# The first routing stage of a macaron block on one core: earlier rows of the second token group, the first group's residual on VectorE, paired statistics, fewer warm-up products

## The chip, the cores and the metric

The kernel runs on one core of a Trainium2 chip. The core has TensorE (PE: matrix products; PEld is its weight load), VectorE (DVE), ScalarE (ACT), GpSimd (POOL) and SyncE (SP), which here only issues DMAs. Each engine works through its own instruction list in order and waits on semaphores. The metric is the device time of one execution in microseconds (us). The inputs lie in HBM, and the output goes back there.

## The reference, cut to what matters

The input `x` is 16 x 256 tokens of 256 channels, float32. The block is

```
x = x + 0.5 * ffn(LN(x))     # mixture of experts
x = x + attention(LN(x))
x = x + 0.5 * ffn(LN(x))     # the same weights again

ffn(h):                      # h is LN(x)
  n    = w_norm * h / sqrt(mean(h*h) + 1e-6)
  p    = softmax(n @ w_router)             # 32 experts; the 4 best of each token
  out  = sum over the chosen experts of p * (silu(n@w_gate[e]) * (n@w_up[e])) @ w_down[e]
  out += sigmoid(n @ w_shared_gate) * ((silu(n@sw_gate) * (n@sw_up)) @ sw_down)
  return h + out
```

Since `ffn` returns `h + out`, the first line is `x + LN(x)/2 + out/2`. The change touches the beginning of this first line: the statistics of `LN`, the sum `x + LN(x)/2`, and the order in which rows and weights come in.

## The kernel before

The 4096 tokens are 32 tiles of 128 rows, in 8 groups (g = 0 to 7) of 4 tiles. All of `x` stays in one on-chip tile `x` [128, 32, 256].

**Loads.** SP issues in this order: group 0 of `x` in two halves (`load_x(0, 2)`, L116), the identity matrix `kc` (L119), `wnorm` (L134), the router's weights `wr` (L136, L137), the shared expert's gate and up weights `sw` in four pieces (gate columns 0 to 639, gate 640 to 703, up 0 to 639, up 640 to 703; L144, L145), group 1 of `x` (L146, recorded as L116), the down weights `swd` (L148, L151), then groups 2 to 7 of `x` (L153). All of them go through one hardware queue.

**Routing of a group,** `route(n, g, rows)` (n = 0 is the first feed-forward), is a generator, and each `yield` lets other work in between:

1. `moments(g)`: for each tile `bn_stats` (L221) and `bn_aggr` (L222) on DVE give mean and variance `mv`. `root` on POOL (L228, then a power of -1/2 at L229) turns the variance into `s2` (for the normed rows) and `s1` (for the LayerNorm). POOL then makes the factors `xa` (L242) and `xb` (L244, L245) of `x + LN(x)/2 = xa*x + xb`.
2. DVE writes the normed rows `xr` (L250), 4 instructions.
3. Twice (h = 0, 1): PE transposes two tiles of `xr` into PSUM (`pt`, L267), and ACT scales them into `xnT` (L270).
4. `mixed()` writes `x = xa*x + xb` over `x`, 4 instructions of ACT (L258). It overwrites `x`, so it stands after `xr`. For the first group it is written after the router's exponential (L294), for the other groups between the two halves of step 3.
5. PE makes the router's logits `pl` (L283). DVE, ACT and DVE again make the softmax, the four best experts and the mask (L287 to L316). The table of rows `xtab` goes to HBM (L308).

**The shared expert of a group,** `shared`, is what PE is filled with in the meantime: for each of 6 column chunks k, gate and up products into two PSUM tiles `pg` (L402, `sw` times `xnT`), a tanh on ACT (L407; L430 for the last chunk), and two products on DVE (L408 and L420; L432 and L433 for the last chunk). Then the down products `po` (L457) for four tiles, each added to `x` by DVE (L461). `po` needs all six chunks `act`.

**What sets the order.** PE runs in the order in which the code is written (`tc.manual_schedule(engines={ET.PE})`, L101). On DVE, ACT, POOL and SP a planner orders the first stage: it goes through the program once with costs of its own and gives each engine the earliest written instruction that it believes to be ready. The list is then fixed; on the chip an instruction that waits holds up everything behind it on its engine. A `manual_schedule` region for DVE fixes the written order among the DVE instructions in it, and leaves to the planner where other DVE work falls between them.

**Warm-up.** `warm(count)` issues products of zeros on PE (L190): 9 before the first transposes, and 3 between the transposes of group 0 and its logits (`WARM = (9, 3)`, L739 and L740). Each float32 product shows as two records in the profile.

In `feed_forward` (L728) the written order for g = 0 is: first half of step 3 for group 0, `moments` of group 1, second half of step 3, `xr` of group 1, the warm-up, logits of group 0 and their softmax, `moments` of group 2; after that the first chunk of the shared expert. `advance(first[0], 2)` (L791) has written steps 1 and 2 of group 0 before that.

Of the kernel before, what the change touches and what calls it, by code (L numbers as in the profile page):

```python
# [9 lines left out]
F32 = mybir.dt.float32  # L10
BF16 = mybir.dt.bfloat16
I32 = mybir.dt.int32
AF = mybir.ActivationFunctionType
ALU = mybir.AluOpType
# [4 lines left out]
P = 128  # L19
# [3 lines left out]
GT = 4  # L23
# [16 lines left out]
ET = mybir.EngineType  # L40
# [3 lines left out]
ROUTE_FILL, SLOT_FILL, FIRST_FILL, EXPERT_FILL, SUM_FILL, PROJECT_FILL = 3.0, 1.7, 6.0, (2.15, 2.3), 17.0, 1.5  # L44
LAST_FILL = 8.0
MASK_FILL, ROW_FILL = 4.0, 3.2
WARM = (9, 3)
AHEAD = 3
SPARE = (0.0, 0.0, 2.0, 3.0)
LAST = 4 * (NG - 1)  # L50
# [43 lines left out]
def macaron_kernel(ctx: ExitStack, tc: tile.TileContext, X, Wq, Wk, Wv, Wo, w_norm, w_router, w_gate, w_up,  # L94
                   w_down, sw_gate, sw_up, sw_down, w_shared_gate, consts, out):
    nc = tc.nc
# [14 lines left out]
    x = cpool.tile([P, NT, C], F32, name="x")  # L111

    def load_x(g, parts=1):
        for i in range(g * GT, (g + 1) * GT, GT // parts):
            j = i + GT // parts
            nc.sync.dma_start(x[:, i:j, :], xf[i * P : j * P, :].rearrange("(t p) c -> p t c", p=P))  # L116
# [23 lines left out]
    sw = cpool.tile([P, 2, 2 * FS], F32, name="sw")  # L140
    swv = [w.rearrange("(c p) f -> p c f", p=P) for w in (sw_gate, sw_up)]
    f0 = FC[-1][0]
    for s in range(2):
        nc.sync.dma_start(sw[:, :, s * f0 : (s + 1) * f0], swv[s][:, :, 0:f0])  # L144
        nc.sync.dma_start(sw[:, :, 2 * f0 + s * FR : 2 * f0 + (s + 1) * FR], swv[s][:, :, f0:FS])  # L145
    load_x(1)  # L146
    swd = cpool.tile([P, len(FC), C], F32, name="swd")
    nc.sync.dma_start(swd[:, 0:5, :], sw_down[0:640, :].rearrange("(c p) d -> p c d", p=P))  # L148

# [66 lines left out]
    def moments(g):  # L216

        mv = stat.tile([P, GT, 2], F32, name="mv", bufs=5)
        for t in range(GT):
            st = stat.tile([P, 6], F32, name="st")  # L220
            nc.vector.bn_stats(st, x[:, g * GT + t, :])  # L221
            nc.vector.bn_aggr(mv[:, t, :], st)  # L222
        return mv

    def root(name, mv, scale, add):
# [6 lines left out]
    def route(n, g, rows):  # L232

        mv = moments(g)


        s2 = root("s2", mv, 1.0 + RMS_EPS, RMS_EPS * LN_EPS)
        s1 = root("s1", mv, 1.0, LN_EPS)  # L240
        xa = stat.tile([P, GT], F32, name="xa", bufs=5)
        nc.gpsimd.tensor_scalar(xa, s1, 0.5, 1.0, ALU.mult, ALU.add)  # L242
        xb = stat.tile([P, GT], F32, name="xb", bufs=5)
        nc.gpsimd.tensor_mul(xb, s1, mv[:, :, 0])  # L244
        nc.gpsimd.tensor_scalar_mul(xb, xb, -0.5)  # L245
        yield 0.0
        xr = rows.tile([P, GT, XW], F32, name="xr", bufs=2 if n else 3)
        for t in range(GT):
            i = g * GT + t
            nc.vector.tensor_scalar(  # L250
                xr[:, t, 0:C], x[:, i, :], mv[:, t, 0:1], s2[:, t : t + 1], ALU.subtract, ALU.mult
            )
        yield 0.0

        def mixed():
            for t in range(GT):
                i = g * GT + t
                nc.scalar.activation(  # L258
                    x[:, i, :], x[:, i, :], AF.Identity, bias=xb[:, t : t + 1], scale=xa[:, t : t + 1]
                )  # L260

        for h in range(GT // 2):
            pt = ps1.tile([P, 2, 2, P], F32, tag="mm", name="pt")
            for j in range(2):
                t = 2 * h + j
                for c in range(2):
                    nc.tensor.transpose(pt[:, c, j, :], xr[:, t, c * P : (c + 1) * P], ident)  # L267
            i0 = (g * GT + 2 * h) * P
            for c in range(2):
                nc.scalar.activation(  # L270
                    xnT[:, c, i0 : i0 + 2 * P], pt[:, c].rearrange("p j t -> p (j t)"), AF.Identity,
                    scale=wnorm[:, c : c + 1],
                )
            yield 0.5
            if h == 0:
                if n or g:
                    mixed()
                yield 0.0
        pl = ps1.tile([P, GT, E + 1], F32, tag="mm", name="pl")
        for t in range(GT):  # L280
            i = g * GT + t
            for c in range(2):
                nc.tensor.matmul(  # L283
                    pl[:, t, :], lhsT=xnT[:, c, i * P : (i + 1) * P], rhs=wr[:, c, :], start=(c == 0), stop=(c == 1)
                )
        lg = stat.tile([P, GT, E + 1], F32, name="lg", bufs=2)
        nc.vector.tensor_copy(lg, pl)  # L287
        nc.vector.tensor_copy(gate[:, g * GT : (g + 1) * GT], lg[:, :, E])
        mx = stat.tile([P, GT, 1], F32, name="mx")
        nc.vector.tensor_reduce(mx[:, :, 0], lg[:, :, 0:E], AX.X, ALU.max)  # L290
        ex = stat.tile([P, GT, E], F32, name="ex", bufs=2)
        nc.vector.tensor_sub(ex, lg[:, :, 0:E], mx.to_broadcast([P, GT, E]))
        yield 1.9
        nc.scalar.activation(ex, ex, AF.Exp)  # L294
        if n == 0 and g == 0:
            mixed()
        yield 0.0
        tot = stat.tile([P, GT, 1], F32, name="tot")
        nc.vector.tensor_reduce(tot[:, :, 0], ex, AX.X, ALU.add)
        nc.vector.reciprocal(tot, tot)  # L300

        pr = stat.tile([P, GT, E + 4], F32, name="pr", bufs=1)
        nc.vector.memset(pr[:, :, E : E + 4], -1.0)
        nc.vector.tensor_mul(ex, ex, tot.to_broadcast([P, GT, E]))

        nc.vector.scalar_tensor_tensor(pr[:, :, 0:E], ex, TINY, ex, ALU.is_ge, ALU.mult)
        nc.gpsimd.tensor_copy(xr[:, :, C:XW], pr[:, :, 0:E])
        nc.sync.dma_start(xtab[n][g * GW : (g + 1) * GW, :].rearrange("(t p) c -> p t c", p=P), xr)  # L308
        top = stat.tile([P, GT, 8], F32, name="top")
        hit = stat.tile([P, GT, E + 4], F32, name="hit", bufs=1)  # L310
        for t in range(GT):
            nc.vector.max(top[:, t, :], pr[:, t, 0:E])
        nc.vector.memset(top[:, :, TOPK:8], -1.0)
        for t in range(GT):
            nc.vector.match_replace(hit[:, t, :], top[:, t, :], pr[:, t, :], 2.0)
        nc.vector.tensor_single_scalar(  # L316
            mask[:, :, g * GT : (g + 1) * GT], hit[:, :, 0:E].rearrange("p t e -> p e t"), 1.5, ALU.is_gt
        )
        yield 0.0
# [360 lines left out]
    def advance(work, count=1):  # L680
        for _ in range(count if work else 0):
            next(work, None)
# [45 lines left out]
    def feed_forward(n, pool, works, fill, routed=None):  # L728


        for g, work in works.items():
            later = [works.get(g + d) for d in range(3)]
            next(work)
            if g == 0:
                next(later[1])
            fill.take(ROUTE_FILL)
            advance(work, 2)
            advance(later[1])
            if n == 0 and g == 0:  # L739
                warm(WARM[1])  # L740
            fill.take(ROUTE_FILL)
            advance(work, 2)
            advance(later[2])
            fill.ready = g + 1
            fill.take(ROUTE_FILL)
            next(work)
        if n == 0:
            routed.close()
            clear(0)
            load_attention()  # L750
        idx = pool.tile([P, E], I32, name="idx")
        fill.take(MASK_FILL)
        with tc.tile_pool(name=f"slots{n}", bufs=4, side="right", reuse_waits="tile") as sp:
            works = [slots(sp, idx, q) for q in range(E // 8)]
            for step in range(5):
                for w in works:
                    next(w)
                    fill.take(SLOT_FILL if step < 3 else ROW_FILL)
        fill.take(FIRST_FILL)
        wds = [pool.tile([FE, 2, C], F32, name=f"wd{i}") for i in range(3)]  # L760
        for wd in wds:
            nc.gpsimd.memset(wd[FR:FE, 1, :], 0.0)
        steps = [expert(pool, n, e, idx, wds[e % 3]) for e in range(E)]


        twice = pool.tile([P, C], F32, name="twice")
        for h in range(2):
            nc.sync.dma_start(twice[h * FR : (h + 1) * FR, :], sw_down[640:FS, :])
        fill.paired = twice

        for e in range(AHEAD):
            next(steps[e])
        fill.halves = True
        with tc.manual_schedule(engines={ET.Pool}):
            for e in range(E + 2):
                if e + AHEAD < E:
                    next(steps[e + AHEAD])
                for late in range(3):
                    if 0 <= e - late < E:
                        next(steps[e - late], None)  # L780
                fill.take(EXPERT_FILL[n])
        fill.halves = False
# [4 lines left out]
    with tc.tile_pool(name="ffn0", bufs=1) as pool:  # L787
        rows0 = ExitStack()
        xrows = rows0.enter_context(tc.tile_pool(name="rows0", bufs=3, side="right"))
        first = {g: route(0, g, xrows) for g in range(NG)}  # L790
        advance(first[0], 2)  # L791
        feed_forward(0, pool, first, fill, rows0)
        if n == 0:
            fill.paired = None
# [174 lines left out]
```

## Time and profile before

| | us |
|---|---|
| median of 3 runs (lowest to highest) | 1030.83 (1030.72 to 1031.55) |
| the profiled execution | 1031.41 |
| its span, first to last instruction | 1029.5 |
| PE busy | 1012.2 (98%) |
| DVE busy | 640.2 (62%) |
| POOL busy | 496.4 (48%) |
| ACT busy | 410.1 (40%) |

The start of the execution, in stretches (busy us of each engine, DMA as the mean busy share of 16 DMA engines and GB/s):

| stretch, us | PE | DVE | ACT | POOL | DMA share | GB/s |
|---|---|---|---|---|---|---|
| 5 to 10 | 5.00 | 1.68 | 2.23 | 3.21 | 0.98 | 324 |
| 10 to 15 | 4.84 | 2.19 | 3.28 | 0.79 | 1.11 | 335 |
| 15 to 20 | 4.68 | 4.33 | 2.17 | 2.62 | 1.10 | 348 |
| 20 to 25 | 5.00 | 4.36 | 2.75 | 3.22 | 1.02 | 344 |
| 25 to 30 | 5.00 | 4.66 | 2.93 | 0.32 | 0.74 | 199 |
| 30 to 35 | 5.00 | 4.32 | 2.46 | 3.10 | 0.14 | 48 |
| 35 to 40 | 4.71 | 3.60 | 2.04 | 2.41 | 0.84 | 218 |
| 40 to 50 | 7.83 | 9.94 | 3.99 | 5.01 | 0.94 | 292 |
| 50 to 60 | 10.00 | 5.31 | 2.52 | 5.11 | 0.94 | 314 |

A line of the timeline or of the chain begins with the start and the length in us, then the engine, the line of the code and the operation; "x4" is how many instructions were merged, and the bracket at the end of a timeline's line is the idle time before it and what ended it. A line of the waits reads: engine and line that waited, whom it waited for, then the total, the number and the longest wait. A matmul's end is modelled, so a busy PE is not always PE at its best rate.

### The profile page before, as it was taken

Reading aid. Unit: us, or ns where it says so; the run is one execution under the profiler, and the core shown is the slowest. Engines: PE = TensorE matmul, PEld = TensorE weight load, DVE = VectorE, ACT = ScalarE, POOL = GpSimd, SP = SyncE. Lnnn points to the kernel's source line nnn. Section 1 sums busy time; section 2 is a strip of 40 time slices with the busy share of each in tenths; the row PEclk is TensorE's granted clock in tenths of the full one; section 3 lists DMA queues with packets and bytes.
Section 4 is the critical chain, followed back from the end, with each engine's and each line's share of the span. In section 5 each row is a group of like instructions: output and inputs, shape, how many; then the busy total and the mean of one; then the engine's idle time right before and its main releaser. Section 6 shows DMA issues by size and latency. Waiting matters only on the chain.

```text
span 1029.5 us, 15832 instructions
## 1 busy us (share of the span) xinstructions
PE 1012.2 (98%) x5432; PEld 639.4 (62%) x5432; DVE 640.2 (62%) x1698; ACT 410.1 (40%) x896; POOL 496.4 (48%) x548
## 2 busy tenths in 40 slices
PE   9999999999999999999999999999999999999998
PEld 6657646777866464545555554555566477877755
DVE  5865665455453557787878879775755644454553
ACT  4442111223231247676758667667310123232210
POOL 4410101555553389788687767754100235555442
PEclk9999999999999999999999999999999999999999
DMA  9731801788873100000101010000310157788564
GB/s 297 215 125 47 249 8 50 167 176 176 179 159 47 46 22 3 20 21 2 44 1 45 1 44 13 12 24 2 105 33 1 35 119 170 170 174 177 104 174 169
DMA packets 138191, 93.26 MB, mean 91 GB/s; under 512 B 80576, under 2 KB 135424, under 8 KB 138112
## 3 DMA queue, kind: packets, MB, share of 16 engines
q1 hardware_dynamic: 125824, 74.42, 25.8%
q0 software_dynamic: 12288, 17.83, 10.5%
q8 instruction: 44, 0.72, 0.3%
q14 instruction: 35, 0.29, 0.1%
HBM read 61.25 MB, written 30.97 MB: 90 GB/s over the span
## 4 chain that ended last, share of the span: by engine, by line
PE 83%; DVE 7%; DMA 4%; POOL 3%; issue 1%; ACT 1%; SPq 0%; POOLq 0%; DVEq 0%
PE pg L402 26%; PE po L457 8%; PE pge L492 7%; PE pq L558 7%; PE poe L505 5%; PE poa L673 5%; PE sc L607 5%; PE pos L457 4%; PE y L655 3%; PE den L655 3%; PE pv L586 3%; DMA acc<-y,idx 2%; PE pl L283 2%; PE pte L484 1%; DVE xr L250 1%
## 5 line engine op out<-in xcount | busy, mean ns | idle before, releaser
L402 PE MATMUL pg<-xnT,sw 128*128 128x512 f32 x704 | 320.7, 596 | 0.5 <-DVE act L427 0.5
L402 PEld LDWEIGHTS pg<-xnT,sw 128*128 128x128 f32 x704 | 129.9, 190 | 130.6 <-issue 121.1
L508 POOL DMA_INDIRECT acc<-y,idx x64 | 101.4, 1584 | 178.1 <-DVE y L507 83.0
L407 ACT ACTIVATE act<-pg 128x512 f32<-128x512 f32 (+1 forms) x94 | 52.9, 563 | 206.4 <-PE pg L402 198.4
L614 ACT ACTIVATE p<-sc 128x512 f32<-128x512 f32 (+1 forms) x256 | 105.0, 497 | 74.9 <-PE sc L607 74.8
L408 DVE SCALAR_TENSOR_TENSOR act<-act,pg 128x512 f32<-128x512 f32 (+1 forms) x94 | 60.7, 646 | 80.1 <-ACT act L407 79.7
L457 PE MATMUL po<-swd,act 128*128 128x256 f32 x432 | 102.4, 385 | 4.4 <-ACT x L258 1.8
L468 POOL DMA_INDIRECT xg<-xtab,idx x64 | 68.1, 1064 | 73.9 <-DVE idx L377 55.0
L619 ACT ACTIVATE p<-p 128x512 f32<-128x512 f32 (+1 forms) x128 | 102.3, 867 | 0.0
L621 POOL TENSOR_SCALAR_AFFINE_SELECT p<-p 128x512 f32<-128x512 f32 x128 | 83.4, 676 | 36.6 <-ACT p L619 35.2
L492 PE MATMUL pge<-xgT,wgu 128*112 128x128 f32 (+1 forms) x768 | 95.0, 273 | 0.7 <-DVE sie L500 0.7
L457 PEld LDWEIGHTS po<-swd,act 128*128 128x128 f32 x432 | 79.6, 190 | 22.6 <-issue 6.0
L492 PEld LDWEIGHTS pge<-xgT,wgu 128*112 128x112 f32 (+1 forms) x768 | 88.9, 182 | 1.9 <-issue 1.9
L487 ACT ACTIVATE xgT<-pte,wnorm 128x128 f32<-128x128 f32 x128 | 40.0, 365 | 108.7 <-PE pte L484 108.7
L420 DVE TENSOR_TENSOR act<-act,pg 128x512 f32<-128x512 f32 x80 | 54.9, 687 | 29.7 <-PE pg L402 28.8
L498 DVE SCALAR_TENSOR_TENSOR sie<-sie,pge 112x256 f32<-112x256 f32 x64 | 27.0, 421 | 69.4 <-ACT sie L497 69.3
L566 POOL TENSOR_TENSOR qs<-qs,kc 128x512 f32<-128x512 f32 x48 | 61.4, 1280 | 9.8 <-DVE qs L561 9.8
L505 PE MATMUL poe<-wd,sie 112*128 112x256 f32 x256 | 66.0, 380 | 0.0
L457 PE MATMUL pos<-swd,act 128*128 128x256 f32 x280 | 63.8, 380 | 0.0
L673 PE MATMUL poa<-wo,yT 128*128 128x256 f32 x256 | 60.0, 386 | 1.4 <-DVE qT L565 1.4
L558 PE MATMUL pq<-hT,wq 128*128 128x512 f32 x128 | 60.9, 600 | 0.0
L607 PE MATMUL sc<-qT,kT 32*128 32x256 f32 (+1 forms) x512 | 59.9, 533 | 0.0
(118 smaller groups left out, 1478.5 us busy)
## 6 DMA issues: line engine op xcount, KB each, us to landing
xtab<-xr SPq DMA_DIRECT2D x16, 576.0 KB, 3.3
acc<-zero SPq DMA_DIRECT2D x2, 4224.0 KB, 15.9
a<-acc SPq DMA_DIRECT2D x16, 512.0 KB, 7.0
wgu<-in_L_ffn_w_gate SPq DMA_DIRECT2D x64, 112.0 KB, 2.7
wgu<-in_L_ffn_w_up SPq DMA_DIRECT2D x64, 112.0 KB, 2.9
wd<-in_L_ffn_w_down SPq DMA_DIRECT2D x64, 112.0 KB, 2.9
wgu<-in_L_ffn_w_gate SPq DMA_DIRECT2D x64, 64.0 KB, 2.8
wgu<-in_L_ffn_w_up SPq DMA_DIRECT2D x64, 64.0 KB, 2.8
```

The lines of the kernel that those rows point to most:

```text
L402: nc.tensor.matmul(pg[s], lhsT=sw[:, c, at[s] : at[s] + P], rhs=xnT[:, c, cols], start=(c == 0), stop=(c == 1))
L457: nc.tensor.matmul(po, lhsT=act[:, k, t * P : (t + 1) * P], rhs=swd[:, k, :], start=(k == 0 and paired is None), stop=(k == rest if paired ...
L468: nc.gpsimd.indirect_dma_start(out=xg, out_offset=None, in_=xtab[n], in_offset=bass.IndirectOffsetOnAxis(ap=idx[:, e : e + 1], axis=0), bo ...
L492: nc.tensor.matmul(pg[:fw, n_, :], lhsT=wgu[:, c, w0 : w0 + fw], rhs=xgT[:, c, :], start=(c == 0), stop=(c == 1))
L505: nc.tensor.matmul(po, lhsT=si[:, k, :], rhs=wd[:, k, :], start=(k == 0), stop=(k == 1))
L508: nc.gpsimd.indirect_dma_start(out=acc[n], out_offset=bass.IndirectOffsetOnAxis(ap=idx[:, e : e + 1], axis=0), in_=y, in_offset=None, boun ...
L558: nc.tensor.matmul(pq, lhsT=weights[:, c, :], rhs=hT[:, c, :], start=(c == 0), stop=(c == 1))
L607: nc.tensor.matmul(sc[i][:, 0 : 2 * w].rearrange("p (s t) -> p s t", s=2), lhsT=kT[r, m, t0 + k0 : t0 + k0 + P], rhs=qT[r, m, :, t0 + T - ...
L614: nc.scalar.activation(dst[:, i].rearrange("p s t -> p (s t)"), sc[i][:, 0 : 2 * w], AF.Tanh, scale=QK_SCALE / SOFTCAP)
L619: nc.scalar.activation(parts[h], parts[h], AF.Exp, scale=SOFTCAP)
L621: nc.gpsimd.affine_select(out=diag, in_=diag, compare_op=ALU.is_ge, fill=0.0, base=0, pattern=[[0, 4], [1, P]], channel_multiplier=-1,)
L673: nc.tensor.matmul(po, lhsT=yT[:, c // 2, c % 2, qh * P : (qh + 1) * P], rhs=wo[:, c // 2, c % 2, :], start=(c == 0), stop=(c == 3),)
```

## The change

1. `sw` comes in six pieces: columns 0 to 127 of gate and of up; then group 1 of `x`; then columns 128 to 639 of both; then 640 to 703 of both. Two DMAs more in all, the same bytes.
2. `moments` takes the tiles two at a time: two `bn_stats`, then two `bn_aggr`.
3. `mixed` of group 0 in the first feed-forward is 4 `tensor_scalar` of VectorE in place of 4 activations of ScalarE, at the same place in the written order.
4. `moments` and `xr` of group 0, its first transposes, and then `moments` of group 1 are written inside a region that fixes DVE's order. The order in which they were written is the same as before.
5. The second warm-up is 1 product, not 3.

```diff
-WARM = (9, 3)
+WARM = (9, 1)
...
     for s in range(2):
-        nc.sync.dma_start(sw[:, :, s * f0 : (s + 1) * f0], swv[s][:, :, 0:f0])
+        nc.sync.dma_start(sw[:, :, s * f0 : s * f0 + P], swv[s][:, :, 0:P])
+    load_x(1)
+    for s in range(2):
+        nc.sync.dma_start(sw[:, :, s * f0 + P : (s + 1) * f0], swv[s][:, :, P:f0])
+    for s in range(2):
         nc.sync.dma_start(sw[:, :, 2 * f0 + s * FR : 2 * f0 + (s + 1) * FR], swv[s][:, :, f0:FS])
-    load_x(1)
...
-        for t in range(GT):
-            st = stat.tile([P, 6], F32, name="st")
-            nc.vector.bn_stats(st, x[:, g * GT + t, :])
-            nc.vector.bn_aggr(mv[:, t, :], st)
+        for h in range(0, GT, 2):
+
+            sts = [stat.tile([P, 6], F32, name="st") for _ in range(2)]
+            for d, st in enumerate(sts):
+                nc.vector.bn_stats(st, x[:, g * GT + h + d, :])
+            for d, st in enumerate(sts):
+                nc.vector.bn_aggr(mv[:, h + d, :], st)
...
-                nc.scalar.activation(
-                    x[:, i, :], x[:, i, :], AF.Identity, bias=xb[:, t : t + 1], scale=xa[:, t : t + 1]
-                )
+                if n or g:
+                    nc.scalar.activation(
+                        x[:, i, :], x[:, i, :], AF.Identity, bias=xb[:, t : t + 1], scale=xa[:, t : t + 1]
+                    )
+                else:
+
+                    nc.vector.tensor_scalar(
+                        x[:, i, :], x[:, i, :], xa[:, t : t + 1], xb[:, t : t + 1], ALU.mult, ALU.add
+                    )
...
-            next(work)
-            if g == 0:
-                next(later[1])
+            if n or g:
+                next(work)
...
-        advance(first[0], 2)
+
+        with tc.manual_schedule(engines={ET.DVE}):
+            advance(first[0], 3)
+            next(first[1])
```

## The prediction, made before the changed kernel was run

> **What bounds the kernel.** I read the page's shares first, then PE's waits in the first 60 us, then the chain that ended last in that stretch.
>
> ```profile
> PE 1012.2 (98%) x5432; PEld 639.4 (62%) x5432; DVE 640.2 (62%) x1698; ACT 410.1 (40%) x896; POOL 496.4 (48%) x548
> ```
>
> PE is busy nearly always: whatever the change brings must show as PE starting earlier or standing less, and all of PE's idle time is 1029.5 - 1012.2 = 17.3 us. The change touches only the beginning. PE's waits there (engine, line, whom it waited for, us in total, times, longest):
>
> ```profile
> PE po L457 <- ACT x L258: 1.8, 1, 1.8
> ...
> PE po L457 <- DVE x L461: 0.6, 2, 0.3
> ...
> PE pt L267 <- DVE xr L250: 0.3, 1, 0.3
> ...
> PE pl L283 <- ACT xnT L270: 0.2, 1, 0.2
> ```
>
> That is 2.9 us (10 to 60 us: 0.16 + 0.32 + 0.29 + 2.17 by the stretches). It looks as if PE alone set the pace, but the chain says otherwise (start, length, work):
>
> ```profile
> 5.87 6.19 DMA x<-in_L_attn_X
> 12.08 0.75 DVE st L221 x2
> ...
> 14.60 1.05 POOL s L229
> 15.67 1.38 DVE xr L250 x4
> ...
> 17.92 0.67 DVE st L221 x2
> ...
> 20.75 2.03 POOL s L229 x2
> 23.56 0.60 ACT x L258
> ...
> 37.95 1.05 POOL s L229
> 39.02 0.73 DVE xr L250 x2
> 39.75 0.59 DVE act L432
> 40.58 0.69 DVE act L433
> ...
> 49.16 2.86 PE po L457 x12
> ```
>
> From 5.87 to 49.16 no link is PE. The chain begins with the DMA of group 1's rows, landing at 12.06, and goes round statistics (DVE), power (POOL), `xb`, ACT, products (DVE), next statistics. PE has just enough written work to stay busy until 39.7; there it stands 1.8 us, because `po` needs the last chunk, which DVE finishes at about 41.2 (0.59 us of L432 behind an `xr` that waited 1.40 us for POOL). The wait's label, ACT, is misleading: L433 is what ends then.
>
> **Part 1, group 1's rows earlier.** 1408 KB of `sw` go ahead of these rows now, 256 KB after the change, so 1152 KB fewer. The last piece of `sw` was issued at 5.36 and took 5.2 us, so it landed at 10.56; the 512 KB of rows followed at 12.06: 341 KB per us. 1152/341 = 3.4, hence landing at 8.7. Bounds: not before 4.84 (its new issue slot) + 2.9 (a 256 KB piece of `x`) = 7.7; not after 12.06 - 1.03 (two issue slots of 0.51 earlier) = 11.0. I take 8.7, since in this stretch the DMA share is 0.98 to 1.12: the queue moves bytes and waits for no issue.
>
> The page "DMA: Bandwidth & Descriptors" of the Trainium skill (Bandwidth, "Measured") speaks against the split: it asks for transfers of 1 MiB and gives about 2.0 us plus bytes over 436 GB/s for one. Were that paid one after another, the estimate for two pieces of 128 KB and the rows would be 2.3 + 2.3 + 3.2 = 7.8 us from 3.82, landing at 11.6, and little would be won. The four pieces of `sw` say no: by that sum they need 11.3 us, and they took 6.7, so the fixed parts overlap.
>
> DVE is free at 8.48 (end of group 0's `xr`). Statistics of four tiles took 3.47 to 5.29, 1.82 us, already in pairs there; so the pairing is worth 0 for group 0 (the same order), and for others between -0.4 (12.08 to 13.97 was 1.9, but with other work inside) and +0.4; I take 0. From the start of the statistics to `xr` took 12.08 to 15.67 = 3.6: `xr` at about 12.3, instead of 15.67, **3.4 us earlier**.
>
> **What is late next: group 2's rows.** The last two groups landed at 12.9 + 9.0 = 21.9 and 14.5 + 8.9 = 23.4, 1.5 us a group; four groups back, group 2 lands at 15.9. The bytes ahead of it do not change (two more issues, 2 x 0.47 us on SP, lie beside a full queue: 0, at most +0.9). Its statistics began at 17.85; now at 15.9 at the earliest, ending 1.82 later, 17.7. POOL began the root at 20.20, so here the lead is **2.4 us**.
>
> **Part 2, `mixed` on DVE.** Four instructions like `xr` (same tile, same two scalars): 4 in 1.38. The rows are `xr`; bounds 0 (idle gap) to +1.4 (on the chain). Does it fit? From 8.5: statistics 1.8, `mixed` 1.4, `xr` 1.4, logits' copies and maximum 0.7, the difference 0.3, `sg` 0.2, L408 0.7, L420 0.65: 7.1, ending at 15.6, just before 15.9. The cover is DVE's idle 8.48 to 12.08 and 14.3 to 15.67; without it, 1.4 of the 2.4 us is lost. Behind a waiting `mixed` (its `xb` is ready at 9.02) would stand group 1's `xr`; both come after that time anyway.
>
> **Part 3, ACT freed and the warm-up cut.** ACT now does this at the start:
>
> ```profile
> 7.58 1.28 ACT L258 ACT_TABLE_LOAD   x1 [7.58 <-DVE xr L250]
> 9.05 0.60 ACT L258 ACTIVATE x<-x,xb,xa 128x256 f32<-128x256 f32 x1 [0.18 <-POOL xb L245]
> 9.55 0.82 ACT L270 ACTIVATE xnT<-pt,wnorm 128x256 f32<-128x256 f32 x2
> ```
>
> The first `xnT` stands behind one `mixed`. Group 0's first four transposes end at about 8.4 (8 in 1.13 from 7.84); so `xnT` can run 8.45 to 9.3, and the logits start at 9.35 instead of 10.43. The two products removed are 4 of 6 records in 1.46 us: the warm-up ends at 9.3, not 10.27, so it no longer holds them. PE gains 1.08, and the 0.32 at 16.23 goes as well (`xr` is there at 12.7, needed at 14.8): **1.4 us** for PE.
>
> The table load is the doubt. Its first instruction will be `xnT`. In the rows above the load passed while `xb` was still missing (the activation behind it waited 0.18 for POOL), so it is not held by its activation's last wait; then it runs under the wait for the transposes and costs 0. At the other end it starts after them, 8.45, and `xnT` begins at 9.75: the logits at 10.65, PE's gain 0.1. I take 0. The skill's "ScalarE: Activation LUTs" ("What happens when an `exp` ACTIVATE runs") puts the load right before the activation that needs it, and "What ACT_TABLE_LOAD costs" gives about 2.66 us with its drain. By that figure the logits would start at an estimated 12.0, PE 1.6 us late; the row has 1.28 and an activation 0.19 after it.
>
> **Part 4, the fixed order.** It names the order that DVE ran anyway: 0. Bounds come with the rivals.
>
> **Sum.** The chain from 17.7 on is 2.4 us early, through POOL, ACT and L408 to L433, unless PE's `pg` comes too late for it. ACT's tanh ran 0.2, 2.1, 2.9, 1.4, 2.8, 1.0 us behind the product it reads (chunks 0 to 5); the chain's lead over PE is 2.4 - 1.4 = 1.0, so it fits from chunk 1 on, the last one exactly. PE reaches the stall at 39.7 - 1.4 = 38.3 and goes on at 41.53 - 2.4 = 39.1: stall 0.8 instead of 1.8. Behind that PE is full (40.00 of 40 us from 180 to 220 and 220 to 260) and nothing is tied to the clock on the wall, so the shift passes through. 1031.41 - 2.4 = 1029.0 for the profiled execution, which lies 0.58 above the median: **1028.4**. About 0.2% (2.1 us) is what a measurement here can tell from no change; the forecast lies just beyond it.
>
> **Rivals.**
>
> A, the forecast: the chain moves, 1.4 (only PE's gain) to 2.8 us. Chance 0.50, a third of it under 2.06.
>
> B, the stall at 41.5 vanishes: with its `xr` no longer ahead of L432 (the order is planned anew), PE alone sets the pace, and gains 1.4 + 0.29 + 2.17 = 3.9 at most, 3.4 likely: 1027.4. For it: one stall on one misplaced `xr`; against it: the same planner places it. Chance 0.17.
>
> C, the head start is hidden: `mixed` costs its 1.4 on the chain and the table load keeps PE at 0.1; or the first stage is early but a later root gives the rest back. 2.4 - 1.4 - 1.0 = 0: 1030.8, within 0.6 below and 1.1 above. For it: DVE is 87 to 93% busy from 15 to 30. Chance 0.16.
>
> D, slower: DVE gets late in the replanned order. An `xr` placed too early holds DVE until POOL's power is done: 1.40 us a time, seen twice (14.27 and 37.62). Had `mixed` its 1.4 on the chain and three more of the groups 2 to 7 such a hold, 1.4 + 3 x 1.4 = 5.6, less 2.4: +3.2, **1034.0**. It decides from the third hold on (two give +1.8). For it: the change reorders all of DVE's first stage; against it: before, four groups of six had none. Chance 0.17.
>
> **Numbers.** Faster: 0.33 of A and B's 0.17, 0.50. Same: 0.17 of A and C, 0.33. Slower: D, 0.17. Range: low end B's floor, 1030.83 - 3.9, rounded to 1026.9; high end C's upper bound, 1031.9; left out is D.
>
> **To look for.** Group 1's statistics begin at about 8.7 and its `xr` at 12.3; group 2's statistics at 15.9; the logits at 9.35; the table load before 8; the `po` stall near 39 under 1 us. Wrong if group 1 lands after 10.8 (PE then waits), if the load follows the transposes, or if DVE idles on POOL in more than two groups.

## The result and the profile after

The changed kernel takes 1038.32 us (median of 14 runs, 1032.27 to 1041.91) against 1031.98 (14 runs, 1030.72 to 1036.6): ratio 1.0052, interval 1.0038 to 1.0066, so it is **slower by some 5.4 us** (the two medians alone lie 6.3 apart). The forecast was 2.4 us faster, and its range ended at 1031.9. The profiled execution took 1038.26, its span is 1036.3.

In the page of the changed kernel, the line of PE has 3.4 us more than before, though PE has 4 records fewer to run, and the row of the granted clock (40 slices, 9 is 0.9 or more) shows a slice that was full before:

```profile
PE 1015.6 (98%) x5428; PEld 640.8 (62%) x5428; DVE 635.9 (61%) x1702; ACT 408.7 (39%) x892; POOL 495.7 (48%) x548
PEclk9899999999999999999999999999999999999999
```

More busy time for less work means a slower engine. PE's two longest waits of the changed kernel up to 60 us (same columns as in the prediction):

```profile
PE po L470 <- DVE ex L305: 2.2, 1, 2.2
PE pl L296 <- ACT xnT L283: 2.2, 1, 2.2
```

The stall at `po` is there again, no longer 1.8 but 2.2, and a second stall of the same length is new: PE stands in the middle of group 1's logits, waiting for `xnT`. The code is 13 lines further down than before here; L296 is the `pl` of L283, L470 the `po` of L457.

PE's own work at both places (start, length, how many records, two to a float32 product; the bracket is the wait before it):

```profile
22.38 0.97 PE L296 MATMUL pl<-wr,xnT 128*128 128x33 f32 x8
25.51 1.72 PE L296 MATMUL pl<-wr,xnT 128*128 128x33 f32 x8 [2.16 <-ACT xnT L283]
27.04 6.58 PE L415 MATMUL pg<-xnT,sw 128*128 128x512 f32 x8
...
45.81 0.67 PE L470 MATMUL po<-swd,act 128*128 128x256 f32 x2 [2.22 <-DVE ex L305]
```

In the kernel before, the same two pieces of work were:

```profile
24.05 1.87 PE L283 MATMUL pl<-wr,xnT 128*128 128x33 f32 x16
25.75 3.68 PE L402 MATMUL pg<-xnT,sw 128*128 128x512 f32 x8
```

At 22.38 PE is 1.67 us ahead of before (24.05): so far the change does what it should. Then it stands 2.16 us, and the eight `pg` records behind the stand take 6.58 us, where eight took 3.68 before. PE by stretches (length, busy us with its instructions, granted clock, DMA share, GB/s):

```profile
25.00:30.00 5.00, 4.49 (x12) 0.61 0.74 209
30.00:35.00 5.00, 5.00 (x12) 0.71 0.01 2
...
40.00:50.00 10.00, 7.78 (x36) 0.83 0.88 253
```

The clock granted to PE falls to 0.50 from 26.1 for 6.8 us, and after the second stall from 46.5 for 3.4 us. In the kernel before it was 1.00 in all of these stretches.

Why `xnT` came late is in ACT's list (the release of each wait in the bracket):

```profile
15.13 2.08 ACT L266 ACTIVATE x<-x,xb,xa 128x256 f32<-128x256 f32 x4 [5.14 <-POOL xb L252]
...
17.20 0.58 ACT L420 ACTIVATE act<-pg 128x512 f32<-128x512 f32 x1
...
24.50 0.60 ACT L266 ACTIVATE x<-x,xb,xa 128x256 f32<-128x256 f32 x1 [5.32 <-POOL xb L252]
25.00 0.82 ACT L283 ACTIVATE xnT<-pt,wnorm 128x256 f32<-128x256 f32 x2
```

Group 1's four `mixed` (L266) now stand **ahead** of the first tanh (L420). They wait 5.14 us for `xb`, and the tanh starts at 17.20; in the kernel before it started at 14.23 and these four came behind it, at 17.83 and 19.03:

```profile
14.23 0.60 ACT L407 ACTIVATE act<-pg 128x512 f32<-128x512 f32 x1
17.83 1.09 ACT L258 ACTIVATE x<-x,xb,xa 128x256 f32<-128x256 f32 x2 [3.00 <-POOL xb L245]
```

DVE then waits for ACT, and has the two products of the first chunk (17.81 and 18.61) to do before group 2's statistics, which stand behind them:

```profile
17.33 0.17 DVE L402 TENSOR_SCALAR sg<-sg 128x4 f32<-128x4 f32 x1 [1.76 <-ACT sg L401]
17.81 0.69 DVE L421 SCALAR_TENSOR_TENSOR act<-act,pg 128x512 f32<-128x512 f32 x1 [0.31 <-ACT act L420]
18.42 0.28 DVE L312 TENSOR_REDUCE tot<-ex 128x4 f32<-128x128 f32 x1
18.61 0.69 DVE L433 TENSOR_TENSOR act<-act,pg 128x512 f32<-128x512 f32 x1
19.21 0.75 DVE L227 BATCH_NORM_STATS2 st<-x 128x6 f32<-128x256 f32 x2
```

Group 2's statistics begin at 19.21 (before 17.85, forecast 15.9). DVE's own list is new here too: in the kernel before they stood directly behind the first product, ahead of the second:

```profile
17.25 0.68 DVE L408 SCALAR_TENSOR_TENSOR act<-act,pg 128x512 f32<-128x512 f32 x1
17.85 0.74 DVE L221 BATCH_NORM_STATS2 st<-x 128x6 f32<-128x256 f32 x2
...
19.37 0.65 DVE L420 TENSOR_TENSOR act<-act,pg 128x512 f32<-128x512 f32 x1
```

From the first product to these statistics it was 0.60 us and is now 1.40. So of the 1.36 us by which they are later than before, 0.80 is DVE's order, and 0.56 the later first product, which waits for the tanh. The rest is the chain, as the trace follows it:

```profile
21.59 2.02 POOL s L236 x2
...
24.13 0.34 POOL xb L252
24.50 0.60 ACT x L266
25.10 0.37 ACT xnT L283
25.51 1.72 PE pl L296 x8
27.23 6.41 PE pg L415 x8
```

The last link is a head of line: the `mixed` of group 2, which nobody needs soon, waits for POOL, and behind it waits the `xnT` of group 1, whose transposes were done at 19.1. The same order was in the kernel before, but there `xb` came at 23.5 and PE needed `xnT` at 25; now PE is 1.67 us earlier and `xb` is 0.9 us later.

The second stall, at `po`, has the same pattern on ACT. The tanh of the last chunk (L443), whose products PE had done at 39.6, stands behind a `mixed` of group 3:

```profile
42.77 0.60 ACT L266 ACTIVATE x<-x,xb,xa 128x256 f32<-128x256 f32 x1 [3.97 <-POOL xb L252]
43.28 0.58 ACT L443 ACTIVATE act<-pg 128x512 f32<-128x512 f32 x1
```

DVE waits 1.47 us for this tanh, and its last product (L446) ends at 45.56; `po` goes on at 45.81. In the kernel before, an `xr` on DVE made that stall.

**The sum,** up to the start of the last group's logits (100.01 us before, 105.34 after: +5.33; I call it the anchor below, since it takes in the whole stage and nothing behind it):

| from | to | before | after | difference |
|---|---|---|---|---|
| start | logits of group 1 | 24.05 | 22.38 | -1.67 |
| logits of group 1 | logits of group 2 | 11.24 | 17.10 | +5.86: stand 2.16, two windows at half clock 3.4, the break in the logits 0.3 |
| logits of group 2 | logits of group 3 | 16.57 | 17.71 | +1.14: stands 2.22 instead of 2.46 in all, one window 1.4 |

Nothing is added from there to 990 us (+5.04 there); the last 40 us add 1.8 more in this profile, where PE waits 2.6 us for DVE (0.5 before). A window of 3.4 us at half clock does 1.7 us less work. The break is PE's starting anew in the middle of the logits: in run 9 below, where the clock is still full at that place, they take 2.03 us without the stand, and 1.70 in one piece. So of what was lost about 4.8 us is the clock's, 1.9 the stands' and 0.3 the break's, less the lead of 1.67.

### The profile page after: what moved, and what is told of

It reads as the page before. It is cut to its first block, busy times and chain, and to the rows that moved or that the text cites. A ratio compares the mean times of both kernels' runs of the same rounds, so it can differ in the third digit from the quotient of the medians.

```text
span 1036.3 us, 15821 instructions
## 1 busy us (share of the span) xinstructions
PE 1015.6 (98%) x5428; PEld 640.8 (62%) x5428; DVE 635.9 (61%) x1702; ACT 408.7 (39%) x892; POOL 495.7 (48%) x548
## 3 DMA queue, kind: packets, MB, share of 16 engines
q0 software_dynamic: 12288, 17.83, 10.3%
## 4 chain that ended last, share of the span: by engine, by line
PE 87%; DVE 5%; POOL 3%; DMA 2%; issue 1%; ACT 1%; POOLq 0%; DVEq 0%
PE pg L415 26%; PE po L470 9%; PE pge L505 8%; PE pq L571 7%; PE poe L518 5%; PE pos L470 5%; PE poa L686 5%; PE sc L620 5%; PE y L668 3%; PE den L668 3%; PE pv L599 3%; PE pl L296 2%; PE pte L497 1%; PE pa L382 1%; POOL s L236 1%
## 5 line engine op out<-in xcount | busy, mean ns | idle before, releaser
L420 ACT ACTIVATE act<-pg 128x512 f32<-128x512 f32 (+1 forms) x94 | 52.9, 564 | 209.6 <-PE pg L415 199.4
L470 PE MATMUL po<-swd,act 128*128 128x256 f32 x432 | 103.8, 389 | 4.3 <-DVE ex L305 2.2
L470 PEld LDWEIGHTS po<-swd,act 128*128 128x128 f32 x432 | 80.6, 192 | 22.9 <-issue 8.6
L433 DVE TENSOR_TENSOR act<-act,pg 128x512 f32<-128x512 f32 x80 | 54.9, 687 | 29.8 <-PE pg L415 28.7
L470 PE MATMUL pos<-swd,act 128*128 128x256 f32 x280 | 63.8, 380 | 0.0
```

What stands on the lines that cost most here:

```text
L470: nc.tensor.matmul(po, lhsT=act[:, k, t * P : (t + 1) * P], rhs=swd[:, k, :], start=(k == 0 and paired is None), stop=(k == rest if paired ...
```

## The experiments

Twelve runs on three chips, four on each. The kernel before, timed beside them, had medians of 1038.48, 1035.6 and 1037.56 us there, so only ratios are compared, and the anchor in the profiles. My theory was: the planner's order of ACT makes the stall, and the clock makes most of the price. Rivals: DVE is late, by its added work or by its new order (rival D), or one part of the change alone is at fault.

**1. Statistics one tile at a time** (part 2 of the change undone)

```diff
-        for h in range(0, GT, 2):
-            sts = [stat.tile([P, 6], F32, name="st") for _ in range(2)]
...
+        for t in range(GT):
+            st = stat.tile([P, 6], F32, name="st")
+            nc.vector.bn_stats(st, x[:, g * GT + t, :])
+            nc.vector.bn_aggr(mv[:, t, :], st)
```

> The changed kernel with the statistics taken one tile at a time again; everything else of the change stays, the four x + LN(x)/2 on VectorE included. In the planner's list ScalarE now has group 1's second xnT ahead of group 2's first x + LN(x)/2 (in the changed kernel it is behind). Order theory: the 2.2 us stand before the second half of group 1's logits goes, with it the half clock of 26 to 33 us (6.6 us of half speed, about 3.5 us lost); time about 6 us under the changed kernel, 1030 to 1033. VectorE theory (the four instructions added there make it late): VectorE's work is the same, so the stand stays and the time stays at 1036 to 1040.

Ratio 1.0028 (1.0010 to 1.0045), anchor 101.72. PE in this run's timeline:

```profile
23.34 1.87 PE L293 MATMUL pl<-wr,xnT 128*128 128x33 f32 x16
...
41.65 0.67 PE L467 MATMUL po<-swd,act 128*128 128x256 f32 x2 [2.08 <-DVE gate L298]
```

The logits of group 1 run in one piece: the planner put `xnT` ahead of group 2's `mixed` this time. The first tanh is no earlier (18.07). The stall at `po` stays, 2.08, and brings one window at half clock from 43.6. About half of the loss is back, less than the order theory had asked for. Undoing the pairing changed the planner's lists; a price of the pairing as work on DVE is not shown.

**2. The old loads** (part 1 undone: whole pieces of `sw`, then `load_x(1)`)

```diff
-        nc.sync.dma_start(sw[:, :, s * f0 : s * f0 + P], swv[s][:, :, 0:P])
-    load_x(1)
...
+        nc.sync.dma_start(sw[:, :, s * f0 : (s + 1) * f0], swv[s][:, :, 0:f0])
...
+    load_x(1)
```

> The changed kernel with the loads in their old order and pieces (group 1's rows behind all of the gate and up weights). Order theory: in the planner's list group 1's x + LN(x)/2 falls behind the first tanh again, so VectorE gets its products, and with them group 2's statistics, sooner; PE loses the early start instead (it waits about 1 us for group 1's normed rows near 15 us), and the stand before group 1's logits shrinks from 2.2 to under 1 us with no fall of the clock; 1030 to 1033. VectorE theory: the added work has less room than in the changed kernel (statistics of group 1 come 3 us later), so the time is no better than 1037. Theory of the early rows as a pure gain (my prediction): 2 us slower than the changed kernel.

Ratio 1.0032 (1.0013 to 1.0052), anchor 101.79. PE waits 1.33 for group 1's `xr` at 16.39, has no stall in group 1's logits, stands 2.57 at `po`, and one window follows from 42.8. Had the early rows been a pure gain in the changed kernel, this run would be some 2 us behind it; at the anchor it is 3.6 us ahead. ACT's list is that of the kernel before again, though group 0's `mixed` are off ACT here too:

```profile
14.39 0.58 ACT L417 ACTIVATE act<-pg 128x512 f32<-128x512 f32 x1
17.99 1.09 ACT L263 ACTIVATE x<-x,xb,xa 128x256 f32<-128x256 f32 x2 [3.02 <-POOL xb L249]
```

So it takes the early rows, and not the freed place on ACT alone, for the planner to put group 1's `mixed` ahead of the tanh. Group 0's four `mixed` run on DVE at 9.37, while it waits for group 1's rows, and group 2's statistics begin at 18.00 (17.85 before): here their price on the chain is nothing, which is against rival D's price for them.

**3. `mixed` of group 0 on ACT** (part 3 undone)

```diff
-                if n or g:
+                if True:
```

> The changed kernel with the first group's x + LN(x)/2 on ScalarE again. In the planner's list group 1's second xnT stands ahead of group 2's x + LN(x)/2. Order theory: no stand before the second half of group 1's logits, clock full to 40 us; the logits of group 0 start about 1 us later (first xnT behind one x + LN(x)/2 and the table load), time 1030 to 1033. VectorE theory: the same time, but then the gain must show as VectorE's statistics of group 2 starting earlier by the 1.4 us of the four instructions (17.8 instead of 19.2). Time alone does not tell the two apart here; the start of these statistics and ScalarE's order do.

Ratio 1.0034 (1.0012 to 1.0056), anchor 103.43. The window is at another place:

```profile
10.78 1.97 PE L296 MATMUL pl<-wr,xnT 128*128 128x33 f32 x16 [1.02 <-ACT xnT L283]
12.59 5.38 PE L415 MATMUL pg<-xnT,sw 128*128 128x512 f32 x8
```

With ACT busy with `mixed` and only one warm-up product, PE stands 1.02 us ahead of the logits, and from 13.5 for 3.4 us the clock is half (5.38 for eight `pg` records, not 3.68). A second one follows a stand of 2.86 at 50.9. At group 1's logits (25.55) this run is 3.2 us behind the changed kernel, and at the anchor 1.9 ahead, because its list has no stall in these logits. Group 2's statistics begin at 18.61, 0.6 earlier, and not the 1.4 earlier that rival D's price for `mixed` would give; but the first tanh (16.23) is 1.0 earlier too, with one of group 1's `mixed` ahead of it and three behind, so this run does not price `mixed` by itself. None of the three parts, undone alone, gives the time of before back: each new list has a stall of over 2 us at `po`.

**4. ACT held to the written order** in the first stage's routing, all else as changed

```diff
+        routing_order = ExitStack()
+        if n == 0:
+            routing_order.enter_context(tc.manual_schedule(engines={ET.Activation}))
         for g, work in works.items():
...
+        routing_order.close()
```

> The changed kernel with ScalarE's instructions of the first routing stage held to the written order (a region that orders ScalarE in the routing loop of the first feed-forward). The four instructions on VectorE, the early rows and the short warm-up stay. Group 1's x + LN(x)/2 then stands behind the first two tanh, group 2's behind four more chunks. Order theory: tanh of the first chunk at about 13.5 instead of 17.2, statistics of group 2 at 16 instead of 19.2, no stand before group 1's logits and no half clock before 35 us; time 1028 to 1032, under the kernel before by up to 2 us if the stand near 40 us shrinks as predicted. VectorE theory: VectorE keeps its added work, the stand stays, 1036 to 1040.

Ratio 0.9997 (0.9977 to 1.0017), anchor 97.90. From 15.78 ACT's list is:

```profile
15.78 0.58 ACT L420 ACTIVATE act<-pg 128x512 f32<-128x512 f32 x1
16.26 0.83 ACT L283 ACTIVATE xnT<-pt,wnorm 128x256 f32<-128x256 f32 x2
17.14 0.60 ACT L420 ACTIVATE act<-pg 128x512 f32<-128x512 f32 x1
17.63 2.06 ACT L266 ACTIVATE x<-x,xb,xa 128x256 f32<-128x256 f32 x4
```

Two tanh and an `xnT` now come before the four `mixed`; group 2's statistics begin at 17.15 (16 was expected), the stall at group 1's logits is gone, the one at `po` is 1.53, and the profile has a full clock throughout. DVE's work is the same as in the changed kernel, so the added work alone doesn't make the stall. DVE's order is not the same: the planner made it anew, and group 2's statistics stand ahead of the first chunk's second product again. No run changes ACT's list and leaves DVE's as it was. What ties the stall in group 1's logits to ACT is the changed kernel's own trace: its `xnT` had its transposes at 19.1 and stood behind a `mixed` that waited until 24.50, and here it stands ahead and there is no stall. The order of DVE made that `mixed` later by at most the 0.80 us above. The anchor is 2.1 us ahead of before. Over the timed runs that lead doesn't show: of 12 runs, 2 had a mean clock of 1.000, 7 of 0.998 and 3 lower.

**5. The changed kernel once more**, on the second chip

> The changed kernel itself, beside the others of this call. All theories: slower than the kernel before by about 0.5%, with the stand of 2.2 us before the second half of group 1's logits; the last group's logits begin at about 105 us (100.0 in the kernel before). Clock theory: the granted clock halves at least once between 23 and 40 us in the profiled execution, and in nearly every run the mean granted clock is below 1.0.

Ratio 1.0051 (1.0032 to 1.0071), anchor 105.67, the same two stalls (2.45 and 2.23) with half clock from 26.2 for 6.8 us and from 46.7 for 3.4.

**6. Zeros into the stand** (5 products of zeros between the two halves of group 1's logits; order and lateness of ACT stay)

```diff
+            if n == 0 and g == 1 and t == 2:
+                warm(5)
```

> The changed kernel with five products of zeros on PE between the two halves of group 1's logits, just where PE stands 2.2 us; they take about 2.4 us and fill the stand. Clock theory (the stand itself costs 2.2 us, and the half clock that follows it costs some 3.5 us more): the clock stays full from 23 to 40 us, PE is 3 us earlier at 40 us than in the changed kernel, and the time falls by 2 to 4 us. Theory that the order alone costs and the clock is an accident: nothing gained, or 0.3 us lost. The planner's list for VectorE differs a little from group 3 on, since it counts the five products.

Ratio 1.0017 (0.9999 to 1.0035), against 1.0051 of run 5 on the same chip; the anchor is 101.18, 4.5 us better. PE:

```profile
23.66 2.40 PE L194 MATMUL pw<-zero 128*128 128x256 f32 x10
25.90 1.21 PE L298 MATMUL pl<-wr,xnT 128*128 128x33 f32 x8
26.95 3.68 PE L417 MATMUL pg<-xnT,sw 128*128 128x512 f32 x8
```

The logits go on no sooner than in the changed kernel (25.90; 25.51 there), PE does 2.2 us of useless work where it stood, and the eight `pg` records take 3.68 again. From the second half of the logits to group 2's transposes it is 4.56 us, where the changed kernel takes 7.94: 3.4 us are the price of the two windows. By group 2's transposes (30.46, not 33.45) 3.0 us are won by keeping PE busy alone; the rest comes later, where a stand of 2.34 at `po` was not followed by a window. (DVE's list differs from group 3 on, so the second part is not the zeros' alone.) In the timed runs the mean clock is 0.997 to 1.000 here and 0.993 to 0.997 in run 5, so the profile is no exception. This settles the second half: at group 1's logits the clock took more than the stand.

**7. ACT and DVE held to the written order** (as 4, with `engines={ET.Activation, ET.DVE}`)

> As the experiment with ScalarE in the written order, and VectorE held to the written order too in the routing loop. In that list group 3's and 4's xr stand well behind their statistics, and the last chunk's products directly behind their tanh. Order theory: the stand before the down products near 40 us (1.5 us there) goes as well, PE runs without a stand from 9 to 80 us, the last group's logits begin at 96 to 98 us (97.9 with ScalarE alone held, 100.0 before), and the clock does not fall: 3 to 4 us under the kernel before. Rival: a written order on VectorE puts four statistics in a row ahead of a product that PE waits for (its PSUM buffers), so new stands of 0.5 to 1 us come in their place and the gain is that of ScalarE alone or less.

Ratio 0.9986 (0.9965 to 1.0007), anchor 97.17. PE stands 0.33 (`pg` at 19.55) and 0.93 (`po` at 40.41); the `xr` that had waited 1.4 us for POOL ahead of the last chunk is gone from there. The lead over the kernel before is smaller than the 3 to 4 us expected, and the interval does not exclude none.

**8. As 4, and the warm-up of 3 products**

```diff
-WARM = (9, 1)
+WARM = (9, 3)
```

> The changed kernel with ScalarE in the written order and the second warm-up at 3 products again. The two more products take about 1 us between the first transposes and the logits. If the short warm-up is what lets the clock fall in most runs of the version with ScalarE held (10 of 12 runs there had a mean granted clock under 1.0), most runs now have 1.0 and the time is 1 to 2 us lower in spite of 1 us more work; if the stand near 40 us is what lets it fall, as many runs as before are under 1.0 and the time is the same or up to 1 us higher.

Ratio 0.9986 (0.9965 to 1.0006), anchor 98.42: 0.5 us later than run 4, and yet 7 of 12 runs, not 2 of 12, have a mean clock of 1.000.

**9. The changed kernel with the warm-up of 3 products** (that line alone; the first stage's lists of ACT and DVE stay)

> The changed kernel with only the warm-up put back to 3 products; the lists of ACT and DVE in the first stage are the same as in the changed kernel, so this varies the length of PE's stand alone. Clock theory (a stand has to be long enough for the granted clock to fall): the logits of group 0 start about 1.0 us later (near 10.3, not 9.31), group 1's logits are due at about 23.4 and still wait for xnT at about 25.5, so the stand shrinks from 2.16 to 1.0-1.3 us, and the clock stays full there (in one-part-alone runs stands of 0.6 us did nothing, those over 1.8 did): the second group's first transposes near 30.5 instead of 33.45, start of the last group's logits near 102 (before 100.01, changed 105.34), ratio to before 1.001 to 1.003. Order theory without the clock: PE gains nothing or loses nothing, last group's logits stay at 105, ratio 1.005. If a stand of 1.1 us is also enough, two half-clock windows remain and the anchor stays at 105.

Ratio 1.0053 (1.0032 to 1.0074), anchor 103.76. PE:

```profile
25.52 1.22 PE L296 MATMUL pl<-wr,xnT 128*128 128x33 f32 x8 [1.26 <-ACT xnT L283]
26.57 5.38 PE L415 MATMUL pg<-xnT,sw 128*128 128x512 f32 x8
```

The stand shrank to 1.26 as expected, but the clock still fell, for one window and not two. The expectation that the clock stays full after a stand this short was wrong: in the kernel before 1.8 us at `po` did nothing, and 1.26 between logits does. The length of the stand is not what decides; the last section has what fits. The ratio is no better than the changed kernel's, although the anchor is 1.6 us better: this profile has a second window from 44.1, at the stand of 2.29 at `po`, like the changed kernel's, and a third from 1013.5, at a stand of 2.5 near the end.

**10. ACT and DVE in written order, warm-up of 3 products** (7 and 8 together)

> The change with ACT and DVE held to the written order in the first stage, and the warm-up of 3 products instead of 1. Theory (order and clock): nothing of the chain changes against the run with both written; PE's lead of 1.0 us at group 0's logits is given up, the stands that follow shrink by as much (0.33 and 0.93 go to 0 and about 0.3), so the last group's logits start at 97.2-97.9 (97.17 with the short warm-up) and the clock is full from the first product on in more of the runs (7 of 12 or more). Ratio to before 0.997 to 0.9985. Rival (the long warm-up is only 1.0 us lost): the anchor at 98.2, ratio 0.9995.

Ratio **0.9972 (0.9954 to 0.9989)**: faster than the kernel before, some 2.9 us (the medians lie 2.0 apart). Anchor 97.31; 8 of 12 runs have a mean clock of 1.000, 4 have 0.998. PE's waits from 8 to 70 us are these two:

```profile
PE po L470 <- ACT xnT L283: 0.9, 1, 0.9
PE pt L280 <- DVE xr L257: 0.9, 1, 0.9
```

No stall of over 1 us is left there. DVE waits 0.21 us for group 2's rows and begins their statistics at 16.57.

**11. The kernel before, ACT and DVE in written order** (the edit of 7 without the change)

> The kernel before, with nothing of the change, but with ACT and DVE held to the written order in the first stage. If the gain of the run with both written belongs to the change (earlier rows of group 1, mixed on DVE), this one stays at the kernel before: last group's logits at 99.5-101, ratio 0.999 to 1.001, PE's total stand before that 2.5 to 3 us. If it belongs to the order alone, the anchor comes to 97-98 and the ratio to 0.9985. Mixed case: a misplaced xr is gone, which was worth up to 1.8 us at po, but the root of group 2 begins as late as before (20.2): anchor 98.5-99.5. I take the mixed case, 99.

Ratio 1.0015 (0.9996 to 1.0035), anchor 101.22, later than the expected 99. PE stands 0.70, 0.86, 0.83 and 0.93 us. So the written order is no gain by itself: with the late rows, 1.4 us are lost by group 1's logits. The gain of run 10 needs the change; between 11 and 10, which differ by the change without its shorter warm-up, the anchor moves 3.9 us, and the intervals of the two ratios do not meet.

**12. The kernel before, warm-up of 1 product** (part 5 alone)

> The kernel before with one part of the change alone: the second warm-up is 1 product, not 3. ACT's list is the same, so xnT of group 0 is ready at 10.37 as before, and PE stands about 0.9-1.2 us ahead of the logits (0.2 before). Clock theory in its strong form (any stand near the start lets the clock fall): a half-clock window of 3.4 us near 13, the anchor at 101.5-102, ratio 1.002. In the form that the other runs suggest (only a stand of some 1.8 us or more): no window in the profile, anchor 100.0, ratio 1.000, and the number of runs with a full clock about as in the kernel before. I take the second, with a somewhat larger share of runs with one window.

Ratio 1.0030 (1.0009 to 1.0051), where 1.000 was expected. In the profile the first stage is as expected: PE stands 1.02 ahead of the logits (10.57), no window follows, anchor 99.83. The loss in the profile lies behind that: 2.8 us of waits for gathered rows before 360 us, and 2.3 us at `pg` near the end with a window at 1010. They cannot be laid to the warm-up: run 10's profile, from the same chip and with 3 products, has as much of both (4.8 us of such waits over the whole execution against 3.7 here, and 2.6 us at `pg`), and the profile of the kernel before is from another chip. Over the timed runs only 1 of 12 has a mean clock of 1.000, against 14 of 35 of the kernel before (on each of the three chips). Three pairs of kernels differ in these two products alone: before and 12, 4 and 8, 7 and 10. With 3 products 29 of 59 runs have a mean clock of 1.000 (one chip's runs of before counted), with 1 product 8 of 36. A fourth pair, the changed kernel and 9, says nothing: neither has a run of 1.000. So the clock falls more often with the short warm-up; why, and where, stays open: the profiles of 7 and 12 have their only window near the end, and the other runs have no trace.

## Where the prediction was right and where it failed

(The parts are numbered as in the prediction.)

- **Group 1's rows (part 1): right.** The statistics begin at 8.96 (8.7 forecast, and 11.6 by the serial sum that the prediction set aside). `xr` came at 13.07, not 12.3, as DVE's `mixed` ran between the statistics, and in run 10 at 12.75 without that. 3.4 us earlier were forecast, 2.6 came.
- **Group 2's rows: nearly right.** 15.9 was forecast as the landing; run 10, whose DVE waits for them, has 16.57. In the changed kernel no wait shows the landing, since DVE comes to these rows only at 19.21.
- **`mixed` on DVE at no cost (part 2): nearly right.** In runs 2 and 10 all four run while DVE would wait for rows (at 9.37 and 14.98). In the changed kernel three of them stand between group 1's statistics, which took 2.3 us (8.96 to 11.29) where run 10 needs 1.8; POOL's root, `xb` and the four `mixed` of group 1 behind it are later by that half microsecond, not by 1.4. The sum that had DVE's work end at 15.6 left out DVE's wait for POOL ahead of `xr` (1.71 us in run 10, where `mixed` ends at 16.36 and the first chunk's products are still to come).
- **ACT freed (part 3): right for the logits** (9.31, forecast 9.35), and the table load came at 4.94, 1.28 us long, under the wait for PE. The logits at 12.0, estimated from the figure of the Trainium skill's page "ScalarE: Activation LUTs" ("What ACT_TABLE_LOAD costs"), did not come. PE's lead of 1.4 was 1.67 at 22.38.
- **The sum failed**, at "from 17.7 on ... 2.4 us early, through POOL, ACT and L408 to L433". It took ACT's list from the trace of before and moved it. But the change gives the planner another start: with group 1's rows early and group 0's four `mixed` gone from ACT, it put group 1's four ahead of the tanh that DVE waited for. With the rows late it left all four behind (run 2), and with group 0's on ACT it put one ahead (run 3). Group 2's statistics were 3.3 us later than forecast, and the chain 1.4 us later than before; 0.80 of these 1.4 is DVE's new order. I had thought of a new order on DVE only (rival D, "An `xr` placed too early holds DVE"). DVE's waits for POOL behind group 0 were three, 3.3 us, against two and 2.8 before; so the sign "if DVE idles on POOL in more than two groups" came, worth half a microsecond. Slower was that rival's side, and a late DVE a part of it; but the stall was made on ACT, and most of the price by the clock, and neither was in it.
- **The clock was no term at all.** The chain's part, +1.4 instead of -2.4, would by itself have given 2.16 - 1.67, or half a microsecond, at group 1's logits. The sentence that was wrong is "nothing is tied to the clock on the wall, so the shift passes through": a stand in a sparse stretch halves the granted clock afterwards, here at a price of 3.4 and 1.4 us. The profile of before has a full clock from 6.6 us on, and from that I took it for constant.
- **The warm-up's cut** was priced as a gain of PE's 1.08 us. Run 12 and its pairs point to a price that the trace of before had no sign of.
- **The mechanism of the forecast existed**: with ACT and DVE in the written order and the old warm-up (run 10) the ratio is 0.9972, where the forecast's 1028.4 of 1030.83 is 0.9977. That the sizes agree is partly luck: there POOL's root of group 2 begins 1.7 us earlier than before (18.47, not 20.20), not 2.4, PE's lead of 1.1 at group 0's logits is given up, and the stall of the last chunk is gone and not halved, which was rival B's point.

## What to carry to other kernels

Where a planner makes in-order lists, a change to one engine's work, or to when its data is ready, is a change to every list: ask what will move ahead, look for instructions that wait long for something nobody needs soon (`mixed` waiting 5 us for `xb` ahead of a tanh), and hold the written order around the edit if it matters. Price a stand of PE with what the clock takes afterwards, above all where it lies among small products. Zeros put into such a stand can pay for themselves.

## What the runs showed of the clock

In all profiles the stretches at half clock ahead of the last products are 3.4 us long or 6.8, and begin at multiples of 3.41 us after the first full clock (20.5 us, or 6 times 3.41, in the changed kernel and in run 9, though these begin at 5.6 and 6.6). So the clock changes on a grid. The page "TensorE: Matmul & The Clock Gate" of the Trainium skill ("What's actually happening") says the same, a window of 3413 ns that is free-running; its later section ("HAM oscillation") asks only for no idle gaps above some 3.4 us, and there the runs differ: 1.26 us was enough.

What fits all the profiles is not how long PE stands in such a window but how little it streams. A record of 512 columns repeats every 0.43 us (8 in 3.43, from 15.07 to 18.50 in the changed kernel), so a float32 column takes 0.84 ns in a record. The few bf16 records change no row of the table, whether their columns count as much or half. Adding up the columns of each window of the 14 profiles up to the last products:

| streamed in a full-clock window of 3.41 us | followed by half clock |
|---|---|
| under 1.2 us | 16 of 16 |
| 1.23 to 1.33 us | 1 of 5 |
| more (some 4200 windows) | none |

Windows in which PE stood 1.85 to 2.02 us but streamed 1.23 to 1.33 kept the clock in four cases; the window of run 9 with 1.26 us of standing streamed only 0.76, because records of 33 columns fill much of the rest and such a record takes as long as some 135 columns would (0.11 us). That makes group 1's logits a poor place for a stand, and would explain why the stall of 1.82 us at `po` cost nothing more in the kernel before: it lay across two windows, with products of 256 columns around it, and these two streamed 2.1 and 2.0 us. Where the grid lies differs from execution to execution (the first full clock comes at 4.5 to 7.3 us), so one kernel has windows in some runs and not in others. This is a regularity of 14 profiles and agrees with run 6, which put columns into a poor window; no run varied the columns alone.
